# A two-layer graph kernel: edge and pack at two tiles, layer 0's slopes on ScalarE, the last norm behind x1's turns, the last products reordered

## The chip, the cores and the metric

The kernel runs on one core of a Trainium2 chip. A core has five engines that each work through a queue of their own in order: TensorE (PE; its weight loads are shown as PEld), VectorE (DVE), ScalarE (ACT), GpSimd (POOL) and SyncE (SP), which here only issues DMAs. They wait for each other through semaphores. The metric is the device time of one execution in microseconds (us), given as the median of several runs.

## The reference

A graph layer with a mean over neighbours, a residual and a layer norm, and then a graph attention layer with a residual and a layer norm, over N = 4096 nodes of C = 512 channels; the adjacency is 4096 x 4096, int32, with some 32 neighbours in a row.

```python
Ab = A > 0
keep = Ab & (cumsum(Ab, axis=1) <= 64)            # the first 64 neighbours of a row
cnt = keep.sum(axis=1, keepdims=True)
nb_mean = (keep @ X) / maximum(cnt, 1)
xj = leaky_relu(nb_mean @ W_nb.T + b_nb)
xi = leaky_relu(X @ W_line.T + b_line)
x = layernorm(x + xi + where(cnt > 0, xj, 0))      # layer 0
...
Wh = h @ W + bW
e = leaky_relu((Wh @ a1 + b1)[:, None] + (Wh @ a2 + b2)[None, :], 0.2)
e = where(adj > 0, e, -9e15)
x = layernorm(x + softmax(e, axis=1) @ Wh)         # layer 1
```

## The kernel before

Rows are worked in NB = 32 blocks of 128. The whole is one hand-written order: each engine executes its instructions in the order in which the program states them.

**Layer 0, first part (to about 237 us).** For each block, x is turned and multiplied with W_nb and W_line (`linear`, L340). The product with W_nb is kept for all blocks as the sum of a high and a low part (`y_hi`, `y_lo`). The other, with bias, slope and x, is written to DRAM as `own_d[b]`. Beside it the adjacency is coded in 64 chunks of 128 x 2048 (`NCH` = 2 a block): SP loads a chunk (L160), ACT makes its `edge` (L167), DVE runs a scan that counts down the neighbours (`left`, L179) and multiplies (L184), ACT packs the result to bytes (`code`, L202) and POOL writes it to `code_d` (L203). 20 chunks are done in this part.

**Layer 0, second part (237 to 706 us).** For each block i four tiles s (16 products each, L502) multiply the turned code with y_hi and y_lo. A tile's weights `kt` are made by ACT (`make_kt`, L249) two tiles ahead, in three buffers, from a transposing load of `code_d` (`load_kt`, L455). After each tile's products the program puts one step of `finish` for the block before (step g of block i - 1 after tile g of block i), all on DVE: step 0 is L462 (mean and bias) and L465 (the slope), step 1 is L469 (adds `own`) and the statistics (L117 to L121; the reciprocal root on POOL, L123), step 2 the norm (L128) and the write of x1 to DRAM, step 3 two sums for layer 1's scores (L481). `codes_step` adds the remaining 44 chunks at 25/16 a block: load and scan at the end of a tile, and at the next tile `codes_late` puts the edge of the next chunk and the pack of the one before, both together, between `make_kt(s + 2)` and the rest. After the last tile come the four steps of block 31.

**Layer 1, products of x1 (706 to 834 us).** x1 is read back in 32 parts s (`load_turned`, L553, four DMAs each on SP, into four slots of the tile `front`, which also holds W). DVE turns each (`turn_x1`, L566, two buffers), PE multiplies it with W (L786, 8 instructions), DVE adds the bias and, for every second part of a pair, makes four differences (`finish_wh`, L575 to L583). Between these stand, from part 8 on, the first two blocks of attention weights: ACT's mask (L604), DVE's reduction (L607), ACT's score (L596), DVE's row maximum (`greatest`, `shift`), ACT's exponential (L649), and from part 22 on two transpositions and combinations of weights (`turn`, `combine`, L668 to L684). Before part 0 the program finishes the score terms (L756 to L771), which go through DRAM on POOL's queue.

**Layer 1, attention (834 to 1607 us).** For pairs of blocks, seven products of half size instead of eight (`consume`, L707, four banks of PSUM for the seven results), with the weights of the next pair made beside it; `end_low`, `end_top` and `end_row` put the results together, norm and write them.

Of the kernel before, what the change touches and what calls it, by code (L numbers as in the profile page):

```python
# [32 lines left out]
def two_layer_adj_gnn(  # L33
# [41 lines left out]

    two = const.tile([P, 1], F32, name="two")
    nc.vector.memset(two, 2.0)
    steep = const.tile([P, 2], F32, name="steep")
    nc.vector.memset(steep[:, 0:1], -0.5 * STEEP)
    nc.vector.memset(steep[:, 1:2], -1.5 * STEEP)  # L80
    far = const.tile([P, 1], F32, name="far")
    nc.vector.memset(far, FAR)
    neg_half = const.tile([P, 1], F32, name="neg_half")
    nc.vector.memset(neg_half, -0.5)

# [24 lines left out]

    code_d = [dram.tile([P, N // 2], BF16, name=f"code_d{b}") for b in range(NB)]

    def ln_stats(y):
        st = stat.tile([P, nc.vector.BN_STATS_DIM], F32, name="st")
        nc.vector.bn_stats(st, y)  # L117
        mv = stat.tile([P, nc.vector.BN_AGGR_DIM], F32, name="mv")
# [15 lines left out]
    with ExitStack() as l0:  # L134
# [5 lines left out]
        make_identity(nc, ident)  # L140

        late = big.tile([P, 3, C], F32, name="late")
        wa_row, bias_nb = late[:, 0:2, :], late[:, 2, :]

# [77 lines left out]

        def codes_late():

            while late_q:
                q = late_q.pop()
                edge(q + 1)
                pack(q - 1)

        def codes_step(s):  # L230
            while done[0] < min(s, NB * NCH + 1):
                codes_late()
                q = done[0]
                load_adj(q + 2)
                scan(q)
                late_q.append(q)
                done[0] += 1
# [17 lines left out]
        with ExitStack() as la:  # L255
# [9 lines left out]
            def load_turned_x(i):  # L265

                if i < NB:
                    xrs[i] = late[:, i % 3, :].rearrange("p (j c) -> p j c", c=P)
# [44 lines left out]
            rows = []  # L313
            for k in range(2):
                t = early("edge")
                rows += [t[:, c, :] for c in range(NC // 2)]

# [28 lines left out]
            def load_rows(queue):  # L346
                for k, src in enumerate((a1, a2, b_w)):
                    queue.dma_start(rows[k], src.partition_broadcast(P))
                queue.dma_start(b12[:, 0:1], b1.partition_broadcast(P))
                queue.dma_start(b12[:, 1:2], b2.partition_broadcast(P))  # L350

            def fold_w():
                for c in range(NC + 1):
                    wn = raw["w"][c] if c < NC else rows[2]
                    for k in range(2):
                        nc.vector.scalar_tensor_tensor(
                            rows[3], wn, 1.0, rows[k], ALU.mult, ALU.mult,
                            accum_out=wa[:, k, c : c + 1] if c < NC else ca[:, k : k + 1],
                        )
# [91 lines left out]
        def load_kt(b):  # L451
            if b < NB:
                assert done[0] > NCH * (b + 1) and not late_q
                ktbs[b] = ktb_p.tile([P, NT, P], BF16, name="ktb")
                nc.sync.dma_start_transpose(ktbs[b], code_d[b])  # L455

        def finish(i, g):
            if i < 0:
                return
            if g == 0:  # L460
                t = work.tile([P, C], F32, name="t")
                nc.vector.scalar_tensor_tensor(  # L462
                    t, accs.pop(i), rcnt[:, i : i + 1], bias_nb, ALU.mult, ALU.add
                )
                nc.vector.scalar_tensor_tensor(t, t, 0.01, t, ALU.mult, ALU.max)  # L465
                fin[i] = t
            elif g == 1:
                t, y = fin[i], owns.pop(i)
                nc.vector.scalar_tensor_tensor(  # L469
                    y, t, some[:, i : i + 1], y, ALU.mult, ALU.add  # L470
                )
                fin[i] = y, ln_stats(y)
            elif g == 2:
                y, stats = fin[i]
                ln_apply(y, stats)
                nc.gpsimd.dma_start(x1_blk(i), y)
            else:
                y, _ = fin.pop(i)
                for k in range(2):
                    junk = work.tile([P, C], F32, name="junk", bufs=1)  # L480
                    nc.vector.scalar_tensor_tensor(  # L481
                        junk, y, 1.0, wa_row[:, k, :], ALU.mult, ALU.mult,
                        accum_out=e12[:, 1 - k, i : i + 1],
                    )
# [52 lines left out]
    bias_w = ep.tile([P, C], F32, name="res")  # L537
    nc.sync.dma_start(bias_w, b_w.partition_broadcast(P))
# [24 lines left out]
    def turn_x1(s):  # L563
        if s < NS:
            x1ts[s] = ep.tile([P, C], F32, name="c").rearrange("p (m i) -> p m i", i=P)
            nc.vector.transpose(  # L566
# [4 lines left out]
    def finish_wh(s):  # L571
# [121 lines left out]
    def consume(q):  # L693
# [7 lines left out]

        order = (1, 2, 4, 7, 5, 6, 3) if q < NP * NT - 1 else (1, 2, 6, 7, 5, 4, 3)
        for n in order:
# [23 lines left out]
    def end_low(g):  # L727

        p = banks[g]
        top = ep.tile([P, 2, HC], F32, name="c")  # L730
        low = ep.tile([P, 2, HC], F32, name="c")
        nc.scalar.copy(top[:, 0], p[1])
# [20 lines left out]


    cnt, idle = cnts[:, 0, :], cnts[:, 1, :]
    nc.vector.tensor_tensor(cnt, cnt, idle, ALU.add)  # L756
# [15 lines left out]


    for s in range(4):
        load_turned(s)
    load_nat(0, 0)
    load_nat(0, 1)
    turn_x1(0)
    turn_x1(1)
    for s in range(NS):  # L780
        if s > 0:
            load_turned(s + 3)
        pws[s] = ps_acc.tile([P, C], F32, name="acc")
# [18 lines left out]
        if s in (FIRST + 14, FIRST + 18):  # L802
            q = (s - FIRST - 14) // 4
            turn(q)
            combine(q)
    finish_wh(NS - 1)

    for q in range(NP * NT):
# [17 lines left out]
        if b < NB:  # L826
            shift(b)
            for i in range(NI):
                weigh(b, i)
        if k == 0 and g > 0:  # L830
            end_weights(g - 1)
            end_low(g - 1)
            end_top(g - 1)
        if k == 1:
# [43 lines left out]
```

## Time and profile before

| | |
|---|---|
| median of 3 runs (lowest, highest) | 1620.12 us (1619.28, 1620.49) |
| profiled execution | 1619.29 us |
| its span, from the first to the last instruction | 1617.5 us |
| mean granted clock of TensorE | 0.996 |
| PE / DVE / ACT / POOL busy | 98% / 82% / 56% / 16% |
| idle time of PE put down to waits, L786 and L502 | 14.9 us and 3.1 us |

The profile lists for every instruction its start, its duration, and the idle time of its engine before it with what ended it (the releaser). Busy shares are means over the whole span; what a stage is bound by is read from that stage alone. A stretch's granted clock is the share of full speed that TensorE was given. By stage (us, then busy us and count of instructions of PE, PEld, DVE, ACT and POOL, the granted clock, the DMA engines' share and GB/s):

```profile
237.00:614.00 377.00, 374.56 (x1648) 308.45 (x1646) 349.13 (x427) 261.47 (x221) 89.11 (x89) 1.00 0.74 210
614.00:706.00 92.00, 90.98 (x400) 74.96 (x400) 69.19 (x106) 47.47 (x40) 11.65 (x21) 1.00 0.44 129
706.00:714.00 8.00, 0.62 (x1) 0.50 (x2) 6.85 (x18) 0.23 (x1) 2.14 (x3) 0.73 0.63 182
714.00:835.00 121.00, 113.82 (x261) 49.25 (x260) 84.95 (x171) 32.19 (x42) 4.91 (x10) 0.99 0.33 82
835.00:1607.00 772.00, 772.00 (x3578) 679.60 (x3578) 608.61 (x1208) 441.88 (x616) 34.30 (x60) 1.00 0.14 42
```

### The profile page before, as it was taken

The page shows a single profiled execution, that of the slowest core. Times are in us where ns is not written, and L with a number is a line of the kernel's source. Part 1 is how long each engine was busy: PE and PEld are TensorE (multiplying, and loading weights), DVE is VectorE, ACT ScalarE, POOL GpSimd, SP SyncE. Part 2 cuts the span into 40 slices and gives each one's busy share as a digit, 9 for nine tenths or more (in the row PEclk, how much of TensorE's full clock was granted, in tenths as well). Part 3 has the DMA queues.
Part 4 walks back from the last instruction along what each step waited for, and adds up shares of the span by engine and source line. Part 5 has one row for each costly group of instructions (what it writes and reads, how often), then busy time and mean ns, then how long its engine had stood idle before and what let it go on. Part 6 is the DMA issues. An engine that isn't in the chain of part 4 may idle for free.

```text
span 1617.5 us, 18487 instructions
## 1 busy us (share of the span) xinstructions
PE 1584.3 (98%) x6456; PEld 1220.1 (75%) x6456; DVE 1328.7 (82%) x2183; ACT 902.5 (56%) x1054; POOL 257.7 (16%) x395
## 2 busy tenths in 40 slices
PE   9999999999999999989899999999999999999997
PEld 5444448888888787854358888888888888888886
DVE  4999987999999999847787778788888788788763
ACT  2655556677676766413337555567555567555520
POOL 4455532222222221120000000000000000000000
PEclk9999999999999999999999999999999999999999
DMA  8887878767776876352311111111111111111100
GB/s 194 282 260 240 260 210 241 217 196 210 220 212 194 217 205 187 92 130 79 92 46 27 53 40 53 40 27 53 53 40 53 40 28 52 53 40 53 40 7 33
DMA packets 168205, 192.74 MB, mean 119 GB/s; under 512 B 101376, under 2 KB 134176, under 8 KB 159920
## 3 DMA queue, kind: packets, MB, share of 16 engines
q1 hardware_dynamic: 147968, 131.51, 30.1%
q0 software_dynamic: 19712, 59.27, 10.7%
q8 instruction: 50, 0.82, 0.2%
q10 hardware_dynamic: 432, 0.79, 0.1%
q14 instruction: 43, 0.35, 0.1%
HBM read 132.65 MB, written 42.08 MB: 108 GB/s over the span
## 4 chain that ended last, share of the span: by engine, by line
PE 70%; DVE 20%; DMA 4%; issue 3%; ACT 2%; POOL 1%; SPq 0%; POOLq 0%; DVEq 0%; ACTq 0%
PE acc L707 34%; PE pt L707 14%; PE acc L340 9%; PE acc L502 9%; DVE left L179 8%; PE acc L786 4%; DVE left L184 2%; DVE junk L481 2%; DMA a<-in_adj_dram 1%; DVE st L117 1%; DVE own L469 1%; DMA late<-in_x_dram 1%; DVE t L465 1%; DVE t L462 1%; POOL rs L123 1%
## 5 line engine op out<-in xcount | busy, mean ns | idle before, releaser
L502 PE MATMUL acc<-y_hi,kt 128*128 128x512 f32 x1016 | 396.0, 390 | 3.1 <-ACT kt L249 3.1
L502 PE MATMUL acc<-y_lo,kt 128*128 128x512 f32 x1016 | 395.3, 389 | 0.0
L707 PE MATMUL acc<-bt,s 128*128 128x256 f32 x1536 | 342.3, 379 | 0.0
L707 PEld LDWEIGHTS acc<-bt,s 128*128 128x128 f32 x1536 | 291.8, 190 | 39.7
L604 ACT ACTIVATE w<-nat,far 128x1024 f32<-128x1024 uint8 x128 | 136.9, 1135 | 291.6 <-DVE a L668 238.9
L123 POOL TENSOR_TENSOR rs<-ve,neg_half 128x1 f32<-128x1 f32 x64 | 76.0, 1187 | 1026.5 <-DVE ve L121 1026.5
L707 PE MATMUL acc<-bt,a 128*128 128x256 f32 x1024 | 231.6, 379 | 0.0
L707 PE MATMUL pt<-bt,a 128*128 128x256 f32 x1024 | 231.5, 379 | 0.0
L502 PEld LDWEIGHTS acc<-y_hi,kt 128*128 128x128 f32 x1016 | 190.7, 188 | 44.9 <-ACT kt L249 5.3
L502 PEld LDWEIGHTS acc<-y_lo,kt 128*128 128x128 f32 x1016 | 190.7, 188 | 39.4
L707 PEld LDWEIGHTS pt<-bt,a 128*128 128x128 f32 x1024 | 194.6, 190 | 26.9 <-issue 0.5
L707 PEld LDWEIGHTS acc<-bt,a 128*128 128x128 f32 x1024 | 194.6, 190 | 26.5
L668 DVE STREAM_TRANSPOSE a<-w 128x1024 f32<-128x1024 f32 x128 | 153.0, 1225 | 59.4 <-ACT w L649 52.7
L167 ACT ACTIVATE edge<-a,steep 128x2048 bf16<-128x2048 int32 x64 | 127.9, 1998 | 104.5 <-DVE left L184 82.4
L249 ACT ACTIVATE kt<-ktb,steep 128x1024 fp32r<-128x1024 uint8 x124 | 139.4, 1147 | 82.0 <-PE acc L502 64.9
L596 ACT ACTIVATE w<-w,st_n 128x1024 f32<-128x1024 f32 x128 | 149.4, 1233 | 50.7 <-DVE m L607 50.7
L607 DVE CUSTOM_DVE_ANT_0 w<-e_n,w 128x1024 f32<-128x1024 f32 x128 | 149.5, 1221 | 4.3 <-ACT w L604 2.9
L649 ACT ACTIVATE w<-w,nm 128x1024 f32<-128x1024 f32 x128 | 145.4, 1137 | 11.3 <-DVE nm L640 11.3
L179 DVE TENSOR_TENSOR_SCAN left<-two,edge 128x2048 bf16<-128x2048 f32 x32 | 141.3, 4417 | 12.0 <-ACT edge L167 10.9
L179 DVE TENSOR_TENSOR_SCAN left<-two,ends,edge 128x2048 bf16<-128x2048 f32 x32 | 143.2, 4476 | 0.0
L786 PE MATMUL acc<-w,c 128*128 128x512 f32 x256 | 113.6, 602 | 14.9 <-DVE c L566 14.9
L202 ACT CAST code<-left 128x2048 uint8<-128x2048 bf16 x64 | 120.6, 1884 | 7.6 <-DVE left L184 7.6
(114 smaller groups left out, 1529.3 us busy)
## 6 DMA issues: line engine op xcount, KB each, us to landing
a<-in_adj_dram SPq DMA_DIRECT2D x64, 1024.0 KB, 6.0
code_d<-code POOLq DMA_DIRECT2D x64, 256.0 KB, 5.3
nat<-code_d SPq DMA_DIRECT2D x256, 64.0 KB, 2.0
own_d<-xb POOLq DMA_DIRECT2D x32, 256.0 KB, 6.0
own<-own_d SPq DMA_DIRECT2D x32, 256.0 KB, 2.7
x_d<-own POOLq DMA_DIRECT2D x32, 256.0 KB, 2.6
w<-x_d SPq DMA_DIRECT2D x128, 64.0 KB, 2.0
res<-x_d SPq DMA_DIRECT2D x32, 256.0 KB, 2.8
```

What stands on the lines that cost most here:

```text
L167: nc.scalar.activation(edge_of[s], loaded.pop(s), AF.Sigmoid, bias=steep[:, 0:1], scale=STEEP, accum_out=cnts[:, h, b : b + 1],)
L179: nc.vector.tensor_tensor_scan(left, two.to_broadcast([P, CH]), e, NEIGHBORS + 2.0 if h == 0 else end, ALU.max, ALU.subtract,)
L249: nc.scalar.activation(kts[s], bytes_.rearrange("p t (i r) -> p t r i", r=2), AF.Sigmoid, bias=steep[:, 1:2], scale=STEEP,)
L340: nc.tensor.matmul(pl, lhs_t[:, k, :], w_t[name][:, k, :], start=(k == 0), stop=(k == NC - 1),)
L502: nc.tensor.matmul(accs[i], kt[:, k // 2, k % 2, :], term[:, j, :], start=(j == 0 and term is y_hi), stop=(j == NB - 1 and term is y_lo),)
L596: nc.scalar.activation(dst, src, AF.Prelu, bias=bias, scale=scale, alpha=0.2)
L604: nc.scalar.activation(w_i, nats[b, i // 2].bitcast(U8)[:, i % 2, :], AF.Relu, bias=far, scale=-FAR)
L607: nc.vector.tensor_tensor_reduce(w_i, e2_n, w_i, 1.0, -3e38, ALU.subtract, ALU.max, m4s[b][:, i : i + 1])
L649: nc.scalar.activation(w_i, w_i, AF.Exp, bias=nms[b][:, i : i + 1], accum_out=z4s[g][:, r, i : i + 1])
L668: nc.vector.transpose(a[:, r].rearrange("p s (i a) -> p i s a", a=SQ), wts[2 * g + r][:, :, ts(k, 8 * SQ)].rearrange("p i (s x) -> p i s x ...
L707: nc.tensor.matmul(banks[g][n], lhs[:, j, :], bt[:, 4 * k + j, rhs, :], start=(k == 0 and j == 0 and n == mate[0]), stop=(k == NP - 1 and ...
L786: nc.tensor.matmul(pws[s], x1t[:, m, :], ws[:, m, :], start=(m == 0), stop=(m == NC - 1))
```

## The change

Five things, in the order of the program:

- `codes_late` takes a number: in a tile of layer 0 it puts one part of what is waiting (an edge or a pack), so the edge and the pack of a step stand at two tiles. `load_kt` puts what is left first where a block's code isn't packed yet.
- The slope of layer 0's neighbour term (L465, DVE) becomes `bend0`, an activation on ACT, at tile 1 of the next block, between `make_kt` and `codes_late`.
- Block 31's `finish` moves from the end of layer 0 to layer 1, behind the first three turns of x1. Its buffers and the first three turned parts come from a new tile `early`, and `own_d[31]` is loaded behind the first 16 loads of x1.
- Turned parts of x1 have three buffers (the pool `rows`, which also takes over `late`) instead of two; they are turned three parts ahead. A load of x1 stands behind the turn that frees its slot. The four differences of a pair are put off (`combine_wh`): one pair at each part from 16 on, except 22 and 26, and the last two behind the first tile of attention.
- The last seven products come in the order 4, 1, 2, 6, 7, 5, 3, and the last two blocks' sums, norms and writes are written out in one order, the upper block's in two halves.

```diff
+    rows = ctx.enter_context(tc.tile_pool(name="rows", bufs=3, reuse_waits="tile"))
+    late = [rows.tile([P, C], F32, name="c") for _ in range(3)]
+    wa_rows, bias_nb = late[0:2], late[2]
...
-        def codes_late():
-            while late_q:
-                q = late_q.pop()
-                edge(q + 1)
-                pack(q - 1)
+        packed = [0]
+        def pack_late(q):
+            pack(q)
+            packed[0] = q + 1
+        def codes_late(n=1):
+            for part, q in late_q[:n]:
+                part(q)
+            del late_q[:n]
 
         def codes_step(s):
             while done[0] < min(s, NB * NCH + 1):
-                codes_late()
+                codes_late(2)
                 q = done[0]
                 load_adj(q + 2)
                 scan(q)
-                late_q.append(q)
+                late_q.extend([(edge, q + 1), (pack_late, q - 1)])
                 done[0] += 1
...
             def load_late():
                 nc.gpsimd.dma_start(bias_nb, b_nb.partition_broadcast(P))
-                nc.gpsimd.dma_start(
-                    wa_row.rearrange("p k c -> p (k c)"),
-                    wa_d.rearrange("k c -> (k c)").partition_broadcast(P),
-                )
+                for k in range(2):
+                    nc.gpsimd.dma_start(wa_rows[k], wa_d[k].partition_broadcast(P))
...
         def load_kt(b):
             if b < NB:
-                assert done[0] > NCH * (b + 1) and not late_q
+                if packed[0] < NCH * (b + 1):
+                    codes_late(2)
+                assert done[0] > NCH * (b + 1)
...
+        spare = []
+        def place(name, bufs=2):
+            if spare:
+                return spare.pop(0)
+            return work.tile([P, C], F32, name=name, bufs=bufs)
+        def bend0(i):
+            if i >= 0:
+                nc.scalar.activation(fin[i], fin[i], AF.Prelu, alpha=SLOPE)
 
         def finish(i, g):
...
             if g == 0:
-                t = work.tile([P, C], F32, name="t")
+                t = place("t")
                 nc.vector.scalar_tensor_tensor(
                     t, accs.pop(i), rcnt[:, i : i + 1], bias_nb, ALU.mult, ALU.add
                 )
-                nc.vector.scalar_tensor_tensor(t, t, 0.01, t, ALU.mult, ALU.max)
                 fin[i] = t
...
             make_kt(s + 2)
+            if g == 1:
+                bend0(i - 1)
             codes_late()
...
             if g == 2:
-                owns[i] = work.tile([P, C], F32, name="own")
-                nc.sync.dma_start(owns[i], own_d[i])
+                if i < NB - 1:
+                    owns[i] = place("own")
+                    nc.sync.dma_start(owns[i], own_d[i])
...
-        for g in range(NS):
-            finish(NB - 1, g)
...
     front = wp.tile([P, NI, NS * SQ], F32, name="w")
+    early = wp.tile([P, NI, NS * SQ], F32, name="w")
...
+    spare += [early[:, i, C:] for i in (0, 2, 3)]
+    owns[NB - 1] = early[:, 1, C:]
...
-            x1ts[s] = ep.tile([P, C], F32, name="c").rearrange("p (m i) -> p m i", i=P)
+            t = early[:, s, :C] if s < 3 else rows.tile([P, C], F32, name="c")
+            x1ts[s] = t.rearrange("p (m i) -> p m i", i=P)
...
         if h == 1:
+            later.append(kk)
+    later = []
+    def combine_wh():
+        if later:
+            b = bt[:, later.pop(0)]
             nc.vector.tensor_tensor(b[:, 4], b[:, 1], b[:, 0], ALU.subtract)
             nc.vector.tensor_tensor(b[:, 5], b[:, 3], b[:, 4], ALU.subtract)
             nc.vector.tensor_tensor(b[:, 6], b[:, 5], b[:, 2], ALU.subtract)
             nc.vector.tensor_tensor(b[:, 1], b[:, 3], b[:, 1], ALU.subtract)
...
-            wts[b] = wp.tile([P, NI, NS * SQ], F32, name="w")
+            wts[b] = early if b == 0 else wp.tile([P, NI, NS * SQ], F32, name="w")
...
-        order = (1, 2, 4, 7, 5, 6, 3) if q < NP * NT - 1 else (1, 2, 6, 7, 5, 4, 3)
+        order = (1, 2, 4, 7, 5, 6, 3) if q < NP * NT - 1 else (4, 1, 2, 6, 7, 5, 3)
...
-            x1rows[b] = ep.tile([P, C], F32, name="res")
+            if b % 2:
+                x1rows[b] = ep.tile([P, C], F32, name="res", bufs=1)
+            else:
+                x1rows[b] = rows.tile([P, C], F32, name="c")
...
+    for s in range(4):
+        load_turned(s)
+    nc.sync.dma_start(owns[NB - 1], own_d[NB - 1])
+    load_nat(0, 0)
+    load_nat(0, 1)
+    for s in range(3):
+        turn_x1(s)
+        load_turned(s + 4)
+    for g in range(4):
+        if g == 1:
+            bend0(NB - 1)
+        finish(NB - 1, g)
...
-    for s in range(4):
-        load_turned(s)
-    load_nat(0, 0)
-    load_nat(0, 1)
-    turn_x1(0)
-    turn_x1(1)
     for s in range(NS):
-        if s > 0:
-            load_turned(s + 3)
...
         if s > 0:
             finish_wh(s - 1)
-        turn_x1(s + 2)
+        turn_x1(s + 3)
+        load_turned(s + 7)
...
         if s in (FIRST + 14, FIRST + 18):
...
             turn(q)
             combine(q)
+        elif s >= FIRST + 8:
+            combine_wh()
     finish_wh(NS - 1)
...
+        while q == 0 and later:
+            combine_wh()
...
-    end_weights(NT - 1)
-    end_low(NT - 1)
-    end_row(NB - 1, nc.scalar)
-    end_top(NT - 1)
-    end_row(NB - 2, nc.sync)
+    p, rz = banks[NT - 1], rzs[NT - 1]
+    top, low = (rows.tile([P, 2, HC], F32, name="c") for _ in range(2))
+    x_top, x_low = x1rows[NB - 2].rearrange("p (h c) -> p h c", h=2), x1rows[NB - 1]
+    stt = nc.vector.scalar_tensor_tensor
+    st = stat.tile([P, 2, nc.vector.BN_STATS_DIM], F32, name="st2", bufs=1)
+    nc.scalar.copy(top[:, 0], p[1])
+    tt(top[:, 1], top[:, 0], p[6], ALU.add)
+    tt(top[:, 0], top[:, 0], p[2], ALU.add)
+    tt(low[:, 0], top[:, 1], p[7], ALU.add)
+    stt(top[:, 0], top[:, 0], rz[:, 0:1], x_top[:, 0], ALU.mult, ALU.add)
+    nc.vector.bn_stats(st[:, 0], top[:, 0])
+    tt(low[:, 1], low[:, 0], p[5], ALU.add)
+    tt(low[:, 0], low[:, 0], p[4], ALU.subtract)
+    y_low = low.rearrange("p h c -> p (h c)")
+    stt(y_low, y_low, rz[:, 1:2], x_low, ALU.mult, ALU.add)
+    low_stats = ln_stats(y_low)
+    tt(top[:, 1], top[:, 1], p[5], ALU.add)
+    stt(top[:, 1], top[:, 1], rz[:, 0:1], x_top[:, 1], ALU.mult, ALU.add)
+    stt(top[:, 1], p[3], rz[:, 0:1], top[:, 1], ALU.mult, ALU.add)
+    nc.vector.bn_stats(st[:, 1], top[:, 1])
+    mv, rs = ln_rs(st)
+    ln_apply(y_low, low_stats)
+    nc.scalar.dma_start(out_blk(NB - 1), y_low)
+    for h in range(2):
+        ln_apply(top[:, h], (mv, rs))
+        (nc.sync, nc.scalar)[h].dma_start(out_blk(NB - 2)[:, ts(h, HC)], top[:, h])
```

`ln_rs` is the second half of `ln_stats` (aggregate, add the epsilon, reciprocal root on POOL). The three constants' tiles become one, with the same five writes.

More of the change, by code (lines that the diff above doesn't have):

```diff
@@ L74, in two_layer_adj_gnn @@
     ps_acc = ctx.enter_context(tc.tile_pool(name="ps_acc", bufs=6, space=PSUM))
[L76 to L84, printed above, removed]
+    few = const.tile([P, 5], F32, name="few")
+    two, steep, far, neg_half = few[:, 0:1], few[:, 1:3], few[:, 3:4], few[:, 4:5]
+    for k, value in enumerate((2.0, -0.5 * STEEP, -1.5 * STEEP, FAR, -0.5)):
+        nc.vector.memset(few[:, k : k + 1], value)
     wa = const.tile([P, 2, NC], F32, name="wa")
@@ L117, in ln_stats, with ln_rs @@
         nc.vector.bn_stats(st, y)
+        return ln_rs(st)
+    def ln_rs(st):
         mv = stat.tile([P, nc.vector.BN_AGGR_DIM], F32, name="mv")
@@ L140, in two_layer_adj_gnn @@
         make_identity(nc, ident)
-        late = big.tile([P, 3, C], F32, name="late")
-        wa_row, bias_nb = late[:, 0:2, :], late[:, 2, :]
         def transpose_to(dst, src_of, n):
@@ L267, in load_turned_x @@
                 if i < NB:
-                    xrs[i] = late[:, i % 3, :].rearrange("p (j c) -> p j c", c=P)
+                    xrs[i] = late[i % 3].rearrange("p (j c) -> p j c", c=P)
                     for n in range(NC):
@@ L312, in two_layer_adj_gnn @@
                 raw["w"] += [t[:, c, :] for c in range(NC // 2)]
-            rows = []
+            early_rows = []
             for k in range(2):
                 t = early("edge")
-                rows += [t[:, c, :] for c in range(NC // 2)]
+                early_rows += [t[:, c, :] for c in range(NC // 2)]
             def load_w(name, src, queues):
@@ L347, in load_rows @@
                 for k, src in enumerate((a1, a2, b_w)):
-                    queue.dma_start(rows[k], src.partition_broadcast(P))
+                    queue.dma_start(early_rows[k], src.partition_broadcast(P))
                 queue.dma_start(b12[:, 0:1], b1.partition_broadcast(P))
@@ L353, in fold_w @@
                 for c in range(NC + 1):
-                    wn = raw["w"][c] if c < NC else rows[2]
+                    wn = raw["w"][c] if c < NC else early_rows[2]
                     for k in range(2):
                         nc.vector.scalar_tensor_tensor(
-                            rows[3], wn, 1.0, rows[k], ALU.mult, ALU.mult,
+                            early_rows[3], wn, 1.0, early_rows[k], ALU.mult, ALU.mult,
                             accum_out=wa[:, k, c : c + 1] if c < NC else ca[:, k : k + 1],
@@ L479, in finish @@
                 for k in range(2):
-                    junk = work.tile([P, C], F32, name="junk", bufs=1)
+                    junk = place("junk", 1)
                     nc.vector.scalar_tensor_tensor(
-                        junk, y, 1.0, wa_row[:, k, :], ALU.mult, ALU.mult,
+                        junk, y, 1.0, wa_rows[k], ALU.mult, ALU.mult,
                         accum_out=e12[:, 1 - k, i : i + 1],
@@ L536, in two_layer_adj_gnn @@
         )
-    bias_w = ep.tile([P, C], F32, name="res")
+    bias_w = ep.tile([P, C], F32, name="res", bufs=1)
     nc.sync.dma_start(bias_w, b_w.partition_broadcast(P))
@@ L729, in end_low @@
         p = banks[g]
-        top = ep.tile([P, 2, HC], F32, name="c")
-        low = ep.tile([P, 2, HC], F32, name="c")
+        top = rows.tile([P, 2, HC], F32, name="c")
+        low = rows.tile([P, 2, HC], F32, name="c")
         nc.scalar.copy(top[:, 0], p[1])
@@ L833, in two_layer_adj_gnn @@
             end_top(g - 1)
+        if q == NP * NT - 1:
+            end_weights(g)
         if k == 1:
```

## The prediction

> **What bounds the kernel now.** I read the page's busy shares first, then the list of TensorE's waits, then the timelines around its gaps.
>
> ```profile
> span 1617.5 us, 18487 instructions
> PE 1584.3 (98%) x6456; PEld 1220.1 (75%) x6456; DVE 1328.7 (82%) x2183; ACT 902.5 (56%) x1054; POOL 257.7 (16%) x395
> ```
>
> ```profile
> PE acc L786 <- DVE c L566: 14.9, 8, 7.7
> PE acc L502 <- ACT kt L249: 3.1, 4, 1.8
> ```
>
> TensorE (PE) is idle for 33 us of 1617.5, so only a gap of PE can be won. 14.9 us lie at the products of x1 (L786), in 8 gaps, the longest 7.7; 3.1 us at layer 0's aggregation (L502); the rest is the start (some 5 us) and the last 10 us, where the last rows are normed.
>
> Timeline of PE in the stage of x1, of SP and of DVE at its start (start, duration, in brackets the idle time before and its releaser):
>
> ```profile
> 768.28 3.70 PE L786 MATMUL acc<-w,c 128*128 128x512 f32 x8 [1.58 <-DVE c L566]
> 772.95 3.70 PE L786 MATMUL acc<-w,c 128*128 128x512 f32 x8 [0.97 <-DVE c L566]
> ```
>
> ```profile
> 705.46 0.35 SPq L538 DMA_DIRECT2D res<-in_L_gnn_bW_dram  x1
> 705.86 7.74 SPq L553 DMA_DIRECT2D w<-x_d  x16
> ```
>
> ```profile
> 705.70 0.75 DVE L462 SCALAR_TENSOR_TENSOR t<-acc,rcnt,late 128x512 f32<-128x512 f32 x1 [8.34 <-PE acc L502]
> ...
> 712.62 1.29 DVE L566 STREAM_TRANSPOSE c<-w 128x512 f32<-128x512 f32 x2
> ```
>
> And of ACT and PE in layer 0:
>
> ```profile
> 609.69 2.01 ACT L167 ACTIVATE edge<-a,steep 128x2048 bf16<-128x2048 int32 x1 [4.52 <-DVE left L184]
> ...
> 614.68 0.50 PE L502 MATMUL acc<-y_hi,kt 128*128 128x512 f32 x1 [1.84 <-ACT kt L249]
> ```
>
> Layer 0's last product ends at 705.66. VectorE (DVE) then norms block 31 from 705.70 to 712.6, and only then turns x1 for PE, which starts at 713.38. SyncE (SP) loads x1 from 705.86 on: the load of the bias ahead of it (705.46) waits for the place that y_hi leaves. The two ACT and PE rows show the other kind of gap: ScalarE (ACT) waits in order at an edge, its kt comes late, PE stalls.
>
> **The start of layer 1.** The turns move ahead of the norm, but the built program keeps bias_w's wait for the second-to-last product of layer 0. So x1's loads start at 705.86 as before: the first four are issued by 707.2 and land after 2.8 (the landing times of these issues are 2.7 to 3.3): 709.95. A turn takes 0.71 (L566), PE starts at 710.7 instead of 713.38, not at 705.7. The next two loads land at 711.2 and 712.9, their turns end at 711.9 and 713.6. DVE then does block 31's norm. Its first step takes 0.75, ACT's bend 0.63 (the like row L376); but own_d31 is now loaded on SP behind the 16 issues of x1: issue 713.6, +0.35, +2.9 landing = 716.9. From there it is what it was from 707.21 (L469) to 712.62, 5.4 us: DVE is free at 722.3. The fourth turn ends at 723.0, and product 3 starts at 723.05; products 0 to 2 are done at 710.7 + 3 x 3.434 = 721.0 (3.434 is the pace of DVE's waits on them, 732.41 to 735.84). Before, product 3 started at 725.55. **Gain 2.5 us**, not 7.7: the norm is now in front of product 3.
>
> [...] The granted clock was 0.72 in the stretch 709.5 to 710.0, 0.50 to 716.5 and 1.00 from 717: product 0 took 5.3 us instead of 3.43, which costs 1.85. [...] The new gap is 5.0 us, [...] by the row of this gap alone, where the drop came 4.1 us after the last product, it surely would. By the row products 0 to 2 end at 722.9, without a drop at 721.0; product 3 waits for its turn until 723.05 either way. I take 0; without that cover it is 1.9.
>
> **The later products of x1.** Product 0 ended at 718.67 and the stage at 834.1; with 31 products at 3.434 that leaves 9.0 us of stalls (gaps and refill). They stem from products 12 to 19, where ACT and DVE work as a chain: mask 1.13, reduction 1.23, score 1.24, exponential 1.13 make 4.71 us a product, and DVE's next turn is queued behind the reduction. Deferring the 4 additions of a finished pair (1.58 us a product) doesn't shorten this chain; a third buffer of turned x1 gives 3.43 us more to live on. I follow the chain with the rows of before, 2.5 us earlier: the reductions of products 12 to 15 start at 758.6, 766.4, 771.1, 775.8; turns 16, 17 and 18 end at 764.1, 768.9 and 773.6, in time for 767.7, 771.1 and 774.6. Turn 19 ends at 778.2 (wanted 778.0). Then greatest and shift (3.1 us) and the first deferred additions come, turn 20 ends at 784.1 where 781.7 was wanted: 2.4 us. From there DVE needs 0.60 + 0.63 + 1.58 = 2.8 us a product and catches up, until the second transposition and combination of weights (5.03 us, at product 26) make turn 30 late by 0.7. With refills 4.0 us of stalls: 723.05 + 29 x 3.434 + 4.0 = 826.6 against 834.1. **Gain 5.0 us** beyond the 2.5; bounds 0 (the chain still decides) and 9.0 (no stall).
>
> **Layer 0.** Per chunk, edge and pack go to two tiles of PE's work (3.64 us each) instead of one, so ACT is held for 2.2 us plus the wait rather than 4.1 plus the wait. That serves the 3.1 us. But the slope (L465, 0.72 with its gap) leaves DVE and comes to ACT as `bend0`, a wait in the middle of ACT's queue: behind it stand an edge or pack and the next kt, for which PE waits. ACT is in order; so is DVE, which waits for bend0 before L469. How late is DVE? Block i's products end at 251.33 + 14.557 i plus the stalls so far (14.557 is 64 of the products that run from 614.68 to 705.66, 400 of them). L462 came 1.0 us after that for block 4, 13.0 for block 15, 15.3 for block 24 (DVE is 94.5 us busy in 500 to 600, and falls behind). In the new order bend0 of block i stands at tile 1 of block i+1, and the kt behind it must be ready when block i+1 ends: 14.56 - 1.15 (kt) - 1.9 (pack) - 0.63 - 0.75 - 0.2 of handoffs = 9.9 us of lateness can be borne; before, an edge or pack waited only for work 2.5 tiles older.
>
> What DVE saves: 0.72 in 28 blocks. What it pays: where no scan stands between the two steps (17 of the 28 in the built order), it idles for bend0, 0.63 and two handoffs: 0.75; the first block once 3.2 more. Up to block 26 the balance is -19.4 + 16.0 = -3.5 us. Its lateness without stalls was 17.6 there (14.5 and the 3.1 stalled), now 14.1; what exceeds 9.9 is PE's stall: 4.2 us for 3.1. **Loss 1.1 us.** This wait is in no row of before. Bounds: a gain of 3.1 if the split does what it can, and a loss of 6 if DVE idles 1.0 us per direct block and ACT's edges add to it; the nearest row is ACT's wait at L167 with PE's stall of 1.84 behind it. I take the worked value.
>
> **The tail.** The order of the last products puts 5 next to last, where 4 stood. DVE's first sum needs the bank of 5 and 6: it started at 1604.30, 3.2 us before PE's end (1607.5), and starts now 1.5 before it, at 1606.0. Then: eight instructions of 256 columns at 0.34 to 0.48, one of 512 (0.78), its statistics (0.73), and so on through the second half's; the last reciprocal root on POOL (0.56 and 0.15 ahead) and two halves of norm come out at +8.3: last issue at 1614.3, where it was 1614.28. **0**, bounds 0.7 either way.
>
> **At nothing.** The deferred additions of the last two pairs go behind the masks of the first tile of the attention stage; they are wanted three tiles (36 us) later, without that cover 3.2. The score terms (e_d, e_n, st_n on POOL's queue) starts 9.7 us later; e_n landed 14 us after e was ready (712.66 to 726.7), so now at 736.3 and st_n at 738.7, wanted at 744.3 and 745.5. Without that slack each us late is a us of PE. Eight nat loads stand 0.4 us later on SP and have 20 us. Loads of x1 follow their own turn and keep the four slots (4 x 0.43 us of issue in 3.43). The row of wa as two DMAs adds one issue of 0.55 on POOL at some 230 us, used at 261. Residual rows and sums keep one block's distance. Attention (835 to 1607) has PE busy for 772.0 of 772.0 us and no wait goes.
>
> **Sum.** -2.5 - 5.0 + 1.1 + 0 = -6.4. The profiled execution took 1619.29 us (its span 1617.5 and 1.8 around it): 1612.9. The median of the runs shown is 0.8 higher, 1620.12; against it, 1613.7. I say 1613.
>
> **Rivals.** (a) *More is won:* the turns never run dry after the start, and the split takes all of layer 0's stalls: -2.5 - 9.0 - 3.1 = -14.6, 1605.5. For it: DVE is only 85 of 121 us busy in the stage. Against it: the chain of 4.71 us is ACT's, and DVE's order ties the turns to it. (b) *Layer 0 gives the gain back:* x1 brings 6 and bend0 costs 5, so 1619 (no change). For it: DVE has next to no idle time in those blocks. (c) *bend0 becomes the bound, slower:* a DVE idling for ACT that waits for PE. It decides when DVE loses over 1.3 us at each of the 17 direct blocks instead of 0.75: its lateness then grows by 10 more, all of it PE's stall; with ACT held at the same time by an edge, 0.7 us a block on 24 blocks is 17 us for 7.5 won: 1629. Against it: every us that PE stalls lets DVE catch up. (d) *The norm isn't hidden:* if own_d31 lands later still, product 3 starts no earlier than before; then only the stalls go: 1616, on the main case's side.
>
> **Chances.** Main case (with d) 0.58, (a) 0.22, (b) 0.13, (c) 0.07. No change is within 0.2% (3.2 us), about what a measurement of this kernel can tell. Faster: 0.58 + 0.22 + a little of (b) = 0.83; same 0.11, slower 0.06. The range 1606 to 1619 takes in most of (a) and half of (b); the main case's own is 1609.5 to 1616.5.
>
> **What would show it.** PE's first L786 product some 5 us after layer 0's last, and a gap of about 2 us before product 3, released by DVE's turn; later gaps of about 4 us in sum, the largest near product 20; at L502 waits of 3 to 6 us on ACT's kt, each behind a bend0 that waited for DVE; no idle stretch of DVE at the start of layer 1 except for own_d31. The prediction is wrong if the loads of x1 come before the last product, if L502's waits vanish, or if they exceed 8 us.

## The result, and the profile after

| | before | after |
|---|---|---|
| median of 5 runs (lowest, highest) | 1620.12 us (1619.28, 1622.26) | 1614.22 us (1613.07, 1615.72) |
| ratio, 95% interval | | 0.996 [0.9947, 0.9974] |
| profiled execution, its span | 1619.29, 1617.5 us | 1615.72, 1613.9 us |

The change is faster by 0.4%, 5.9 us in the medians, where 1613 was predicted. The profiled execution of before is the lowest of its five and that of after the highest, so the two traces differ by 3.6 us only. A second profile of the changed kernel, taken with the last experiments, has a span of 1612.1.

The page's first lines, and from the list of waits TensorE's three of interest (engine and line that waited, whom for; us in total, times, longest):

```profile
span 1613.9 us, 18473 instructions
PE 1585.2 (98%) x6456; PEld 1222.4 (76%) x6456; DVE 1306.2 (81%) x2154; ACT 918.9 (57%) x1086; POOL 256.9 (16%) x396
```

```profile
PE acc L823 <- DVE w L587: 5.5, 1, 5.5
PE acc L521 <- ACT kt L254: 4.8, 5, 1.5
PE acc L823 <- DVE c L587: 3.1, 3, 2.2
```

The 14.9 us at the products of x1 (now L823) have become 5.5 and 3.1, the 3.1 at layer 0's kt have become 4.8. DVE is 22 us less busy and ACT 16 more: that is the slope, and it shows in no time by itself.

**Layer 0.** ACT's timeline around one of the five stalls, and PE's row behind it (start, duration, in brackets the idle time before and its releaser):

```profile
475.10 1.14 ACT L254 ACTIVATE kt<-ktb,few 128x1024 fp32r<-128x1024 uint8 x1
482.35 0.63 ACT L472 ACTIVATE t<-t 128x512 f32<-128x512 f32 x1 [6.11 <-DVE t L479]
482.89 1.88 ACT L202 CAST code<-left 128x2048 uint8<-128x2048 bf16 x1
484.68 2.19 ACT L254 ACTIVATE kt<-ktb,few 128x1024 fp32r<-128x1024 uint8 x2
```

```profile
485.87 0.51 PE L521 MATMUL acc<-y_hi,kt 128*128 128x512 f32 x1 [1.54 <-ACT kt L254]
```

And of DVE, the mean that this bend waits for:

```profile
481.57 0.74 DVE L479 SCALAR_TENSOR_TENSOR t<-acc,rcnt,c 128x512 f32<-128x512 f32 x1
```

Read downwards: the bend waits 6.11 us for DVE's mean (L479), the pack stands behind it though DVE had finished its input at 473.06, and the kt behind both is 1.54 us late for PE.

**The start of layer 1**, on SP, DVE and PE:

```profile
707.23 0.35 SPq L558 DMA_DIRECT2D res<-in_L_gnn_bW_dram  x1
707.62 8.79 SPq L573 DMA_DIRECT2D w<-x_d  x16
716.51 0.38 SPq L789 DMA_DIRECT2D w<-own_d  x1
```

```profile
712.14 0.71 DVE L587 STREAM_TRANSPOSE w<-w 128x512 f32<-128x512 f32 x1 [9.14 <-DMA w<-x_d]
...
719.59 0.75 DVE L485 SCALAR_TENSOR_TENSOR w<-w,e 128x512 f32<-128x512 f32 x1 [2.95 <-DMA w<-own_d]
...
724.88 0.71 DVE L587 STREAM_TRANSPOSE c<-w 128x512 f32<-128x512 f32 x1
```

```profile
712.90 12.23 PE L823 MATMUL acc<-w 128*128 128x512 f32 x24 [5.47 <-DVE w L587]
725.64 55.20 PE L823 MATMUL acc<-w,c 128*128 128x512 f32 x128 [0.50 <-DVE c L587]
781.19 3.70 PE L823 MATMUL acc<-w,c 128*128 128x512 f32 x8 [0.35 <-DVE c L587]
787.12 43.16 PE L823 MATMUL acc<-w,c 128*128 128x512 f32 x96 [2.23 <-DVE c L587]
```

The bias still stands at the head of SP's queue until layer 0 ends, so DVE has been idle for 9.1 us when the first part of x1 lands. Products 0 to 2 (8 instructions each, 24 in the row) take 12.2 us, because the granted clock is at a half until 716.3 (columns: stretch, its length, PE's busy time, the clock, the DMA engines' share, GB/s):

```profile
709.50:710.00 0.50, 0.00 (x0) 0.50 0.34 89
...
712.50:713.00 0.50, 0.10 (x1) 0.50 0.57 158
...
716.00:716.50 0.50, 0.50 (x2) 0.71 0.08 9
716.50:717.00 0.50, 0.50 (x3) 1.00 0.05 7
```

Then one stall of weight is left, 2.23 us before product 20.

Where the 3.6 us of the two profiles come from, by marks read off PE's timeline (a product's mark is the start of its first instruction):

| stretch | before | after | second profile of after |
|---|---|---|---|
| end of layer 0's products | 705.66 | 707.43 | 706.71 |
| from there to product 3 of x1 | 19.7 | 18.2 | 18.5 |
| product 3 to the first product of attention | 108.6 | 104.5 | 103.1 |
| attention, to the end of PE's last product | 773.7 | 773.7 | 773.7 |
| from there to the end of the span | 9.85 | 10.11 | 10.10 |

### The profile page after: what moved, and what is told of

It is laid out like the page before. It is cut to its first block, busy times and chain, and to the rows that moved or that the text cites. A ratio compares the mean times of both kernels' runs of the same rounds, so it can differ in the third digit from the quotient of the medians.

```text
span 1613.9 us, 18473 instructions
## 1 busy us (share of the span) xinstructions
PE 1585.2 (98%) x6456; PEld 1222.4 (76%) x6456; DVE 1306.2 (81%) x2154; ACT 918.9 (57%) x1086; POOL 256.9 (16%) x396
## 3 DMA queue, kind: packets, MB, share of 16 engines
q0 software_dynamic: 19728, 59.27, 10.9%
## 4 chain that ended last, share of the span: by engine, by line
PE 70%; DVE 16%; issue 6%; DMA 4%; POOL 2%; ACT 2%; SPq 1%; POOLq 0%; DVEq 0%; ACTq 0%
PE acc L736 34%; PE pt L736 14%; PE acc L345 9%; PE acc L521 8%; DVE left L179 8%; PE acc L823 5%; DMA a<-in_adj_dram 1%; DVE left L184 1%; DVE junk L497 1%; POOL rs L126 1%; DVE st L117 1%; DVE t L479 1%; DVE own L485 1%; DVE own L131 1%; DMA xb<-in_x_dram 1%
## 5 line engine op out<-in xcount | busy, mean ns | idle before, releaser
L633 ACT ACTIVATE w<-nat,few 128x1024 f32<-128x1024 uint8 x128 | 136.9, 1136 | 279.7 <-DVE a L697 238.3
L126 POOL TENSOR_TENSOR rs<-ve,few 128x1 f32<-128x1 f32 x64 | 73.3, 1145 | 988.0 <-DVE ve L124 987.8
L254 ACT ACTIVATE kt<-ktb,few 128x1024 fp32r<-128x1024 uint8 x124 | 141.0, 1146 | 45.9 <-PE acc L521 37.4
L167 ACT ACTIVATE edge<-a,few 128x2048 bf16<-128x2048 int32 x64 | 127.5, 1992 | 45.6 <-DVE left L184 23.3
L179 DVE TENSOR_TENSOR_SCAN left<-few,edge 128x2048 bf16<-128x2048 f32 x32 | 141.3, 4416 | 11.4 <-ACT edge L167 11.4
L179 DVE TENSOR_TENSOR_SCAN left<-few,ends,edge 128x2048 bf16<-128x2048 f32 x32 | 143.2, 4475 | 0.0
L202 ACT CAST code<-left 128x2048 uint8<-128x2048 bf16 x64 | 120.5, 1882 | 0.0
L345 PE MATMUL acc<-wt_nb,xt 128*128 128x512 f32 x256 | 115.5, 594 | 2.2 <-DVE xt L299 1.6
```

What stands on the lines that cost most here:

```text
L167: nc.scalar.activation(edge_of[s], loaded.pop(s), AF.Sigmoid, bias=steep[:, 0:1], scale=STEEP, accum_out=cnts[:, h, b : b + 1],)
L179: nc.vector.tensor_tensor_scan(left, two.to_broadcast([P, CH]), e, NEIGHBORS + 2.0 if h == 0 else end, ALU.max, ALU.subtract,)
L202: nc.scalar.copy(code.bitcast(U8), seen_of.pop(s))
L254: nc.scalar.activation(kts[s], bytes_.rearrange("p t (i r) -> p t r i", r=2), AF.Sigmoid, bias=steep[:, 1:2], scale=STEEP,)
L345: nc.tensor.matmul(pl, lhs_t[:, k, :], w_t[name][:, k, :], start=(k == 0), stop=(k == NC - 1),)
L633: nc.scalar.activation(w_i, nats[b, i // 2].bitcast(U8)[:, i % 2, :], AF.Relu, bias=far, scale=-FAR)
```

## Experiments

All are edits of the changed kernel, measured beside runs of before on the same chip, 4 to 8 runs each; a ratio is always to before. Two marks tell more than a single span: PE's waits for kt in layer 0, and the stretch from layer 0's last product to the first of attention ("the x1 stretch": 128.3 us before, 122.7 and 121.6 in the two profiles of after). Layer 0's second part, which the edits of layer 0 aim at, began up to 3.3 us apart from profile to profile (its first product came at 239.43 us in one and at 242.72 in another), so spans are not compared across parts.

**e1: the bias loaded behind x1.**

```diff
     bias_w = ep.tile([P, C], F32, name="res", bufs=1)
-    nc.sync.dma_start(bias_w, b_w.partition_broadcast(P))
...
     nc.sync.dma_start(owns[NB - 1], own_d[NB - 1])
+    nc.sync.dma_start(bias_w, b_w.partition_broadcast(P))
     load_nat(0, 0)
```

> The changed kernel with one DMA moved: bias_w's load stands behind the first 16 loads of x1 and own_d31's, instead of ahead of them. Theory (the head of SP's queue costs the start of layer 1): the 20 loads then land before layer 0's last product at E; only the turn itself and the place of y_hi remain, so PE starts product 0 at E + 0.9 instead of E + 5.5, no clock drop, DVE finishes block 31 at E + 9 and product 3 starts at E + 11 instead of E + 18.2: 7 us less, about 1607. Rival (the landing of x1 or DVE's norm is what PE waits for): the gap at product 0 shrinks but a stall of the same size stands before product 3, under 2 us less in all.

1609.22 us, 0.992 [0.9906, 0.9933]. SP and PE in its trace:

```profile
708.96 0.34 SPq L788 DMA_DIRECT2D w<-own_d  x1
709.34 0.43 SPq L789 DMA_DIRECT2D res<-in_L_gnn_bW_dram  x1
```

```profile
709.69 10.57 PE L823 MATMUL acc<-w 128*128 128x512 f32 x24 [0.58 <-DVE w L586]
720.10 55.10 PE L823 MATMUL acc<-w,c 128*128 128x512 f32 x128
```

The 16 loads of x1 are now issued before 693, while layer 0 still runs; the gap of PE is 0.58 instead of 5.47, the clock stays at 1.00 there, and product 3 finds its turn ready. The x1 stretch is 115.4 us. One load had held the queue, for a bias that the change first uses at 725.50.

**e2: own_d31 loaded first.**

```diff
+    nc.sync.dma_start(owns[NB - 1], own_d[NB - 1])
     nc.sync.dma_start(bias_w, b_w.partition_broadcast(P))
...
-    nc.sync.dma_start(owns[NB - 1], own_d[NB - 1])
     load_nat(0, 0)
```

> The changed kernel with only own_d31's load moved ahead of bias_w's, so that it lands before layer 0 ends. Theory: DVE's wait for it (2.95 us before the second step of block 31) goes, but product 3 was only 0.5 us late, because products 0 to 2 ran at half clock: 0.5 us less in runs with the clock drop, up to 2.5 in runs without it; 0 to 2 us in the median. Rival (this wait sets the end of the stage, since the score terms and all later turns are behind it): 3 us less.

1615.54 us, 0.9959 [0.9946, 0.9971]; x1 stretch 122.2. The load was expected to land before layer 0 ends; it is issued at 707.50, when layer 0's products end (707.66), and the loads of x1 behind it start 0.7 us after that end, for 0.2 in the change. L485 no longer waits for it (0.70, for the bend, instead of 2.95), yet product 3 starts 12.9 us after product 0 with no wait at all: with the clock at a half until 718.95, PE itself took that long. In these runs the late load of own_d31 cost nothing that the clock didn't cost anyway.

**e3: the slope back on VectorE, the split kept.**

```diff
             if i >= 0:
-                nc.scalar.activation(fin[i], fin[i], AF.Prelu, alpha=SLOPE)
+                pass
...
+                nc.vector.scalar_tensor_tensor(t, t, 0.01, t, ALU.mult, ALU.max)
                 fin[i] = t
```

> The changed kernel with layer 0's slope back on DVE (no bend0, except that block 31 too has it on DVE); edge and pack stay at two tiles. Theory of the prediction (bend0 is the wait that gives back what the split gains): PE's waits for kt in layer 0 fall from 4.8 us to under 2, the end of layer 0 comes 3 us earlier, 1611. Rival (DVE's load sets the lateness, and bend0 lightens it): DVE has 0.72 more in each block, the waits for kt rise to 6 or more, 1616 or later.

1614.24 us, 0.9948 [0.9934, 0.9961]; waits for kt 2.7 us. So far it looked as if the bend costs 2 us and the split is worth 0.4. The waits don't show everything: layer 0's second part less its waits for kt is 463.7 us here and 462.1 in e10 below, 1.6 us more. Where they come from isn't shown.

**e5: edge and pack at one tile again, the bend kept.**

```diff
-        def codes_late(n=1):
+        def codes_late(n=2):
```

> Edge and pack of a chunk at one tile again, the bend of layer 0's slope stays on ScalarE (the other half of e3). Theory: the split and the bend pull in opposite directions, the split keeps ScalarE's queue short enough that the bend is bearable. Without the split an edge (2.0), a pack (1.9), a bend (0.6) and the next kt stand in one tile's queue, so TensorE's waits for kt at layer 0's aggregation rise from 4.8 us to 8 or more, and the time by 3 us or more over the change's (ratio to before 0.998 to 1.000). Rival: the split does nothing of its own (e3 showed 2.7 against 3.1 before), ScalarE has slack in every tile: waits for kt stay at 4 to 6 us and the ratio at 0.995 to 0.9965.

1611.45 us, 0.9936 [0.9922, 0.995]; waits for kt 1.9 us. Both the theory and the rival fell: without the split the bend doesn't cost, it gains. ACT at the same block as in the fence further up:

```profile
476.36 1.15 ACT L254 ACTIVATE kt<-ktb,few 128x1024 fp32r<-128x1024 uint8 x1
481.82 0.63 ACT L472 ACTIVATE t<-t 128x512 f32<-128x512 f32 x1 [4.31 <-DVE t L479]
482.36 2.18 ACT L254 ACTIVATE kt<-ktb,few 128x1024 fp32r<-128x1024 uint8 x2
```

The bend still waits, 4.31 us, but the kt comes next. Counted in the traces over the 30 bends that a kt of layer 0 follows: in the change 22 have an edge or a pack between them and that kt, here 11.

**e10: neither; e11: both, with the bend behind the edge or pack.** e10 puts e3 and e5 together. e11:

```diff
-            if g == 1:
-                bend0(i - 1)
             codes_late()
+            if g == 1:
+                bend0(i - 1)
```

> Both parts of layer 0 undone in the changed kernel: edge and pack at one tile again, slope on VectorE; the new start of layer 1, x1 and the end stay. It completes the square of four (split or not, bend on ScalarE or not), of which three waits for kt are known: 4.8 with both, 2.7 with the split alone, 1.9 with the bend alone. Theory: this is before's layer 0, so 3.1 us of waits: each edit alone gains (0.4 and 1.2) and only both together lose; ratio to before 0.9945 to 0.9955, 1 to 2 us faster than the change. Rival: the bend alone was favoured by something else of that run, and the split by itself loses: waits here under 2 us and a ratio as e5's 0.9936.

> Both parts of layer 0 kept, but in its tile the bend is put behind the edge or the pack instead of ahead of it on ScalarE's queue. In the change 22 of 31 bends have an edge or a pack between them and the next kt, without the split only 10. Theory: TensorE's waits come from that order (a bend that waited up to 6.7 us for VectorE holds the pack of 1.9 us too, and the kt behind both is late), so with the bend last the waits fall from 4.8 to 2.5 or less and the ratio to before to 0.994 to 0.995. Rival: it is ScalarE's total work near the end of a block or VectorE's lateness that decides, whatever the order: waits stay at 4 to 5.5 us and the ratio at 0.996.

e10: 1612.31 us, 0.9941 [0.9928, 0.9953], waits for kt 2.9. e11: 1609.87 us, 0.9928 [0.9915, 0.994]. (The counts in its text, 22 of 31 and 10, are 22 and 11 of 30 in the traces.) From the lists of waits of e3, e5, e10 and e11:

```profile
PE acc L522 <- ACT kt L254: 2.7, 4, 1.8
```

```profile
PE acc L521 <- ACT kt L254: 1.9, 2, 1.5
```

```profile
PE acc L522 <- ACT kt L254: 2.9, 4, 1.8
```

```profile
PE acc L521 <- ACT kt L254: 0.5, 1, 0.5
```

| PE's waits for kt | edge and pack at one tile | at two tiles |
|---|---|---|
| slope on DVE | 2.9 (e10; 3.1 before) | 2.7 (e3) |
| bend ahead of them | 1.9 (e5) | 4.8 (the change) |
| bend behind them | not tried | 0.5 (e11) |

By these waits the two interact and don't add: the bend alone is worth 1.0, the split alone 0.2, which is nothing once the 1.6 us that e3 loses beside its waits are counted, both together lose 1.9, and the same two in the other order win 2.4. The whole length of layer 0's second part, with those 1.6 us in e3's, agrees: 465.0 us with neither (e10), 463.4 with the bend (e5), 466.4 with the split (e3), 467.2 with both (the change), 462.0 in e11's order. In e11 ACT makes the same instructions in each tile; only the order differs. The order's effect is shown; its full size isn't separated from VectorE's lateness, which shrinks with PE's stalls.

**e4: the differences made at once.**

```diff
             later.append(kk)
+            combine_wh()
```

> The changed kernel with the four differences of a pair made at once again, as before the change; the third buffer of turned x1 stays. Theory (the chain of mask, reduction, score and exponential ties the turns; DVE idles 2.2 us before each of the reductions of products 13 to 15, which holds the 1.58 of the differences): the stage of x1 takes as long or up to 2 us less, since no backlog stands before turn 20. Rival (putting them off is what won the 4 us): the stage takes 3 to 5 us longer.

1613.88 us, 0.9951 [0.9939, 0.9964]; waits for turned x1 2.3 us, the longest 1.0 instead of 2.2; x1 stretch 120.5. With three turned parts the deferral is no gain: it collects DVE's work where product 20's turn is due.

**e6: turned two parts ahead, the deferral kept.**

```diff
-        turn_x1(s + 3)
-        load_turned(s + 7)
+        if s > 0:
+            turn_x1(s + 2)
+            load_turned(s + 6)
```

> Turns of x1 run two products ahead instead of three, as before the change; the deferred differences, the norm's place and all else stay. Theory: the 4.1 us that the later products of x1 gained come from the third turned row, and the deferral gave nothing (e4): TensorE's waits for turned x1 rise from 3.1 us to 7 or more and the ratio to before rises by 0.002 to 0.003, to 0.998 to 0.999. Rival: the deferral carries the gain and the third row only the start: waits stay under 4.5 us, ratio 0.996 to 0.997.

1617.11 us, 0.9973 [0.9963, 0.9983]; waits for turned x1 5.0 us, of which 1.56 before product 3; x1 stretch 123.0. Between the two expectations, and nearer the rival in the trace: from product 3 to attention it takes 103.9 us where before took 108.6. Either part, the third buffer (e4, 102.7) or the deferral (e6), does nearly all of it. The kernel without both was not run, so what else moved the stage (the loads stand behind their turns now) stays open, as does the rest of the loss in the median beyond the 1.4 us of the x1 stretch.

**e7: the end of before.** The last products in before's order, and its functions for the last two rows.

```diff
-        order = (1, 2, 4, 7, 5, 6, 3) if q < NP * NT - 1 else (4, 1, 2, 6, 7, 5, 3)
+        order = (1, 2, 4, 7, 5, 6, 3) if q < NP * NT - 1 else (1, 2, 6, 7, 5, 4, 3)
...
+    end_low(NT - 1)
+    end_row(NB - 1, nc.scalar)
+    end_top(NT - 1)
+    end_row(NB - 2, nc.sync)
```

> The last products in the order of before (5, 4, 3 at the end) and the last two rows normed by the functions of before; all else as the change. Theory: the new end is worth nothing, or loses 0.2 to 0.5 us (from TensorE's last product to the end 10.2 us against 10.0 before): ratio to before the same as the change's 0.996 within 0.0005, the span's last 10 us are 9.8 to 10.2 after TensorE's end. Rival: the new end wins 1 to 2 us as its shorter chain on VectorE suggests: this kernel is slower than the change by 1 to 2 us, 11 to 12 us after TensorE's end.

1614.66 us, 0.9958 [0.9946, 0.9971]: the same. The last output is issued 6.6 us after PE's last product ends, and 7.1 in the change. The new end's last sums wait for nothing; DVE runs without a wait from 1602.20 to 1609.75 in the change. But it makes 20 instructions in its end (8.3 us of them) where the old end has 17 (7.6), and pays in their count what it gains in order.

**e8 and e9: the findings together.** e8 is e1, e3 and e4; e9 is e1, e5 and e4.

> Three edits on the change together: the bias of x1 loaded behind the first loads of x1, layer 0's slope back on VectorE, the differences made at once. Theory: the three parts lie in three stages (start of layer 1, layer 0, later products of x1) and add: 0.992 from the first, less 0.0012 and 0.0009 from the others, 0.990 of before, 1605 to 1606 us. Waits for kt under 3 us, for the load of x1 under 1 us, for turned x1 about 2.5. Rival: they overlap, since an earlier start finds VectorE and the masks at the same pace later, or the slope on VectorE makes it late for the first turns: 0.9915 to 0.992, no better than the first edit alone.

> Three edits on the change together: the bias of x1 loaded behind the first loads of x1, edge and pack at one tile again with the bend on ScalarE (e5), the differences made at once (e4). Theory: the stages add: 0.9902 (e8) less what the bend alone saves against the slope on VectorE (some 1 us of waits for kt and 0.72 us of VectorE's time a block): 0.9887 to 0.9897 of before, 1603 to 1605 us. Rival: with the earlier start nothing of that is seen at the end: 0.990 to 0.991, as e8.

e8: 1605.76 us, 0.9902 [0.9888, 0.9915]. e9: 1602.67 us, 0.9884 [0.9871, 0.9898], the fastest of all, 18.7 us below the 1621.35 of before in that comparison. Its waits of PE at the three places:

```profile
PE acc L824 <- DVE c L586: 2.3, 3, 1.0
PE acc L521 <- ACT kt L254: 1.9, 2, 1.6
...
PE acc L824 <- DVE w L586: 0.6, 1, 0.6
```

In the traces the three stages add: against the change's second profile the x1 stretch is 113.7 for 121.6 and the waits for kt 1.9 for 4.8, together 10.8 us; the medians differ by 1613.58 - 1602.67 = 10.9. Taken singly the medians promise less: by their ratios against the 0.995 of the change in this comparison, e1, e5 and e4 gain 4.9, 2.3 and 0 us. Where the rest comes from isn't shown. e11's order in e9's place of e5 was not run; by the table it would be worth another 1.4.

The change once more, in that comparison:

> The change itself once more, beside the other kernels of this comparison. Expected: ratio to before 0.996 as in its own result, waits for kt at layer 0's aggregation 4.8 us.

1613.58 us, 0.995 [0.9936, 0.9964], waits for kt 4.8.

## Why the prediction was right, step by step

The sum was -6.4 against the profiled execution; the two profiles of after give -3.6 and -5.4, the medians -5.9. Three of its four parts went the way that was forecast (the fourth was put at 0), but in the first profile each came out less favourable than said; that the medians come within 0.5 us of the sum is in part luck.

- **Layer 0, loss of 1.1:** the waits for kt rose by 1.7 (4.8 for 3.1), by the mechanism named, a bend that waits for DVE with a pack and a kt behind it. The working held in detail. DVE's direct waits were taken as 16.0 us; they are 0.70 at 17 blocks and 4.64 at the first, 16.5 (two more of 4.64 come after the last stall). A lateness of 9.9 us was to be borne: the five stalls stand behind the five bends whose mean started 10.8 to 11.8 us after its block's products, and none stands behind one of 10.2 or less. What was wrong is what the loss was laid to, the bend; e5, e10 and e11 show that the bend gains, and that what loses is the edge or pack which the split puts between the bend and the next kt.
- **Start of layer 1, gain of 2.5:** measured 1.5 and 1.2. That bias_w's wait keeps the loads where they were is shown (e1). PE started 5.5 and 5.1 us after layer 0's end (5.0 said). Product 3 came 18.2 and 18.5 after it (17.4 said), where before it came at 19.7 (725.34 in the trace, 725.55 said). The mis-sized term is SP: the 16 issues took 8.79 us for 7.74 in the first profile. The step that waits for own_d31 (2.95 and 2.9 us) started 12.2 and 11.8 us after layer 0's end for 11.2. The drop of the clock was taken at 0, because the norm would hold product 3 longer anyway. That held in the first profile, where product 3 still waited 0.50 for its turn; in the second its turn was there 0.75 us before PE was. The gap of about 2 us before product 3 that was to show it didn't come, since the drop took 1.7 and 3.0 us of it (products 0 to 2 took 12.2 and 13.5 us, and 10.6 at full clock in e1).
- **Later products, gain of 5.0:** 4.1 and 5.5. The largest stall was put before product 20 with 2.4 us, and is 2.23. The one of 0.7 near product 30 did not come. What the sum didn't hold is a second drop of the clock behind that stall, 1.3 us, in one of the two profiles. That the third buffer does it and the deferral doesn't is half right: e6 shows that the deferral alone does nearly as much.
- **The end, 0:** a loss of 0.26. DVE's first sum started 1.6 us before PE's end and the last issue came 7.1 after it; 1.5 and 6.8 were said, from an end of 1607.5 that is 1607.66 in the trace.
- **At nothing:** held. Attention takes 773.7 us in all three profiles, and no wait of PE for the score terms or the residual rows has appeared.
- **Rivals:** what (a) put on x1, 11.5 us, was there to be won, but by a further edit: e1's x1 stretch is 12.9 below that of before, 8.7 of it ahead of product 3. (b) and (c) did not come: waits for kt stayed under 5 us. Nor did (d): product 3 came earlier, if by less than was said.

## What to carry to other kernels

A step moved ahead is only as early as the head of each queue that it passes: look for the one DMA in front that waits for a place, and put it behind those that don't (e1: PE's gap fell from 5.47 us to 0.58). Where an engine in order must wait for a late one, put the wait last in its slot, behind all work whose inputs are there (e11: PE's waits for kt fell from 4.8 us to 0.5). Test the parts of a change in pairs as well as alone; here an edit that gained and one worth next to nothing lost together, and two that looked like a sum were substitutes.

## What the hardware showed beyond that

After the stall of 2.23 us before product 20 the granted clock fell to a half in the first profile of the change (columns as above):

```profile
787.00:787.50 0.50, 0.38 (x1) 1.00 0.00 0
787.50:788.00 0.50, 0.50 (x2) 0.97 0.00 0
788.00:788.50 0.50, 0.50 (x2) 0.50 0.44 131
788.50:791.00 2.50, 2.50 (x4) 0.50 0.32 91
791.00:791.50 0.50, 0.50 (x2) 0.61 0.44 124
791.50:792.00 0.50, 0.50 (x3) 1.00 0.55 158
```

The fall comes 0.9 us after the gap has ended and lasts for 3.4 us; it costs 1.3 us (43.0 us from product 20 to attention, against 41.7 where the clock didn't fall).

Ten profiles have this stall, of 2.2 to 2.3 us, before product 20 (19 in e6):

| profiles | granted clock behind the stall |
|---|---|
| the first of the change, e1, e11 | fell to a half, for 3.4 us |
| the second of the change, e2, e3, e5, e6, e7, e10 | stayed at 1.00 |

What decides between them isn't shown. Where the clock stayed the stall cost its 2.2 us, where it fell 3.5. The longer gap at the start of layer 1, 5.1 to 6.2 us, brought a fall in all ten profiles that have it (the two of the change, e2 to e7, e10 and e11), as the 7.72 us there did in before; e1's gap of 0.58 us brought none.
